# Reordering a decoder layer's vector and scalar work around its first rows, its group of index 16 and its gate groups

## The chip, the cores and the metric

The kernel runs on one core of a Trainium2 chip. The time is device microseconds for one execution. Before the change the median of three runs is 902.78 us (902.73 to 903.07). One further execution was profiled: it took 903.21 us, of which 901.4 us lie between the first and the last instruction of the core (its span). All durations below come from that one execution.

## What is computed

The reference is one decoder layer in float32 on 16 sequences of 256 rows with 256 channels. Cut to its stages:

```python
# 1. x: 4096 rows; per head of 64 channels a squared-relu attention over two fixed weights
xn = layernorm(x) * g + b
p  = square(relu(xn_heads @ k.T))           # 256 keys, 4 heads
x1 = layernorm(x + (x + p @ v))
# 2. cross attention, 16 heads of 16 channels, 16 batches of 256 queries and 256 keys
D      = clip(frac_k - frac_q, -0.2, 0.2)
logits = gamma * Q @ K.T * scale + delta * (ap * max(D, 0) + an * min(D, 0))
x2     = layernorm(x1 + softmax(logits) @ V @ Wo.T + bo)
# 3. one of 8 experts per row, a low-rank addition to a shared inner layer of 1024
e   = argmax(x2 @ gate.T + gate_b)
out = layernorm(x2 + relu(x2 @ wi.T + wi_b + lora[e]) @ wo.T + wo_b)
```

## The kernel before

All instructions are issued in an order written out by hand; each engine runs its own instructions in that order, and a wait holds back everything behind it on the same engine. The engines are PE (matrix multiply; its weight loads are shown as PEld), DVE (vector), ACT (scalar), POOL (GpSimd) and SP (here it only starts transfers).

**First stage, up to 251 us.** The rows go through in eight blocks of 512 (`rows_in`). `Block.begin` (L271) serves the first block alone. It measures mean and variance of its four tiles of 128 rows on DVE (`row_stats`, L183), takes one inverse root for all four (`scaling`, L234: `near_root`, L192, is a logarithm and an exponential on ACT; `newton`, L199, is three small DVE instructions; `scaling_of`, L238, one more), and then normalises tiles 0 and 1 on ACT (L245) and 2 and 3 on DVE (L283). `turn_first` (L288) transposes the result on PE. Ahead of these transposes stand 30 transposes of the identity (L950) whose result is not used.

**Second and third stage, 251 to 901 us.** The loop at L1062 runs over 64 groups n = 0 to 63, and two steps more. A group is one batch (n // 4) and four of its heads; og = n % 4. In step n the group `now` goes through `logits` (PE, L643, into four PSUM banks `ps_l`) and `maxima` (DVE, L658: adds the negative part of the bias, keeps the row maxima), and then `subtract` (L673) takes the maxima away, the first two heads on POOL and the last two on DVE. The group before it (`last`) is transposed on PE (`turned`, L683) and goes through the exponential on ACT (`exps`, L690), head by head: I call these e0, e1, e2 and e3. The group before that (`older`) goes through `attend` (PE, L699). For the group to come (`nxt`), `negative` (L622 on POOL, L627 on ACT) and `positive` (ACT, L634, one instruction for each bank: s0 to s3) prepare the bias.

Beside this, each step has one large piece of another batch (`pieces`, L721), whose first half is a set of matmuls and whose second half, behind `step(large_piece)`, is the copy out of PSUM:

- og = 0: `queries` (L461), matmuls L465, copied to `qT` by ACT (L481) or, where `vector` is true, by DVE (L476). In steps n = 16, 24, 32, 40, 48 and 56 it is DVE. There `late` (L1171) also puts the copy behind e2 and e3.
- og = 1: `project`. og = 2: `keys`. og = 3: `vals`, matmuls L513, copied by DVE (L521), and `Batch.turned` (L447, transposes L452, copied by ACT at L459).

`divide` (L586, on DVE at L588) scales the attention's output of the batch two before by `invs`, which a transfer has brought from DRAM; it is issued in steps with og = 0, and its result is read by `project` one step later.

From n = 15 on a third strand is woven in, the expert layer of six blocks of rows: `tb, part = divmod(n - 15, 8)`. In part 0 (n = 15, 23, 31, 39, 47, 55) `ff.turn` (L785) transposes normalised rows on PE (L790) in two halves, c0 and c1, each copied by ACT (L793). In part 1 (n = 16, 24, 32, 40, 48, 56, the gate groups) `gates` (L805) and `keep_gates` (ACT, L815) find the expert's scores. Parts 2 and 3 run the large inner matmuls (L878, L890), parts 4 to 7 the outer ones (L908).

Many of the short-lived PSUM tiles come from `tile_b` (L50). From n = 0 on it hands out three buffers in turn, two named B and one named W. So the PE instruction that fills a tile waits until the tile handed out three calls earlier has been copied out. In step 39 the order is e0, e1, `vals`, c0, c1, e2, e3, `Batch.turned`: c1 waits for the exponential of e1, and e2 for the copy of `vals`. From step 16 to 17 it is: gates, e0, e1, `queries`, e2, e3, and then e0 of step 17, which waits for the copy of `queries`.

The order of ACT in part 0 is s0, s1, exponential e0, s2, exponential e1, copy c0, copy c1, s3, exponentials e2 and e3. The parts of the step's text that set it:

```python
if last and n not in (12, 13, 14):
    last.turned(0)
    last.exps(0)
if nxt and n not in (12, 13, 14):
    nxt.positive(2)
if last and n not in (12, 13, 14):
    last.turned(1)
    last.exps(1)
```

Of the kernel before, what the change touches and what calls it, by code (L numbers as in the profile page):

```python
# [11 lines left out]
ALU = mybir.AluOpType  # L12
# [10 lines left out]
def tile_decoder_layer(ctx: ExitStack, tc: tile.TileContext, a: dict, out: bass.AP):  # L23
# [164 lines left out]
    def inv_std(mv, n):  # L188

        return newton(mv, near_root(mv, n), n)  # L190

    def near_root(mv, n):  # L192
        ln = small.tile([P, n], FP, tag="ln", name="ln")
        nc.scalar.activation(ln, mv[:, :, 1], AF.Ln, bias=epst)
        near = small.tile([P, n], FP, tag="near", name="near")
        nc.scalar.activation(near, ln, AF.Exp, scale=-0.5)
        return near

    def newton(mv, near, n):  # L199

        t = small.tile([P, n], FP, tag="sd", name="sd")
        nc.vector.scalar_tensor_tensor(t, mv[:, :, 1], EPS, near, ALU.add, ALU.mult)
        nc.vector.scalar_tensor_tensor(t, t, -0.5, near, ALU.mult, ALU.mult)
        rs = small.tile([P, n], FP, tag="rs", name="rs")
        nc.vector.scalar_tensor_tensor(rs, t, 1.5, near, ALU.add, ALU.mult)
        return rs
# [25 lines left out]
    if True:  # L232

        def scaling(mv, n):  # L234

            return scaling_of(mv, inv_std(mv, n), n)

        def scaling_of(mv, rs, n):  # L238
            nm = small.tile([P, n], FP, tag="nm", name="nm")
            nc.vector.scalar_tensor_tensor(nm, mv[:, :, 0], -1.0, rs, ALU.mult, ALU.mult)  # L240
            return rs, nm

        def scaled(dst, src, by, j):
            rs, nm = by
            nc.scalar.activation(  # L245
                dst, src, AF.Identity, bias=nm[:, j : j + 1], scale=rs[:, j : j + 1]
            )

        class Block:
# [21 lines left out]
            def begin(self):  # L271

                self.xn = p1.tile([P, 4, C], FP, tag="xn", bufs=1, name="xn")
                self.xnT = p1.tile([P, CC, 512], FP, tag="xnT", bufs=1, name="xnT")
                self.mv = small.tile([P, 4, 2], FP, tag="mv", name="mv")
                for jj in range(2):
                    self.measure(jj)
                rs, nm = scaling(self.mv, 4)
                for j in (0, 2, 1, 3):
                    if j < 2:  # L280
                        scaled(self.xn[:, j, :], self.x[:, j, :], (rs, nm), j)
                    else:
                        nc.vector.tensor_scalar(  # L283
                            self.xn[:, j, :], self.x[:, j, :], rs[:, j : j + 1],
                            nm[:, j : j + 1], ALU.mult, ALU.add,
                        )

            def turn_first(self):  # L288
# [126 lines left out]
    if True:  # L415
# [303 lines left out]
        N = len(groups)  # L719

        def pieces(n):  # L721

            b, og = divmod(n, 4)
            ahead, nxt, last, older = (
                batches[b + d] if 0 <= b + d < B else None for d in (2, 1, -1, -2)
            )
            if og == 0:
                return nxt and nxt.queries(n > 15 and n % 8 == 0), None, []
            later = nxt if nxt and nxt.b >= MADE else None
            if og == 1:  # L730
                return older and older.project(), None, [later and (lambda: later.clip("dneg"))]
            if og == 2:
                return nxt and nxt.keys(), None, [later and (lambda: later.clip("dpos"))]
            more = [ahead and ahead.load]
            if ahead:
                more.append(ahead.reload if ahead.b < MADE else ahead.fractions)
            return nxt and nxt.vals(), ahead and ahead.turned(), more

        def step(piece):
            if piece:  # L740
                next(piece, None)
# [201 lines left out]
    with tc.manual_schedule():  # L943
# [18 lines left out]
        by = [None] * (NB + 1)  # L962
# [4 lines left out]
        for tb in range(NB):  # L967
# [3 lines left out]
            mv = small.tile([P, 8, 2], FP, tag="mv8", bufs=2, name="mv8")  # L971
# [3 lines left out]
            if tb > 1:  # L975
                last = rows_in[tb - 2]
# [7 lines left out]
            if tb > 2:  # L984
                older = rows_in[tb - 3]
# [5 lines left out]
            if tb + 1 < NB:  # L991
                nxt = rows_in[tb + 1]
# [69 lines left out]
        for n in range(N + 2):  # L1062
            now, nxt, last, older = (
                groups[n + d] if 0 <= n + d < N else None for d in (0, 1, -1, -2)
            )
            large_piece, small_piece, more = pieces(n)
            tb, part = divmod(n - FIRST, 8)
            ff = rows_out[tb] if 0 <= tb < FUSED or (tb == FUSED and part < 2) else None
# [45 lines left out]
            if halved:  # L1114
                for g in range(2):
                    last.turned(g)
                    last.exps(g)
                if part == 2:
                    ff.route()
                now.subtract((nc.gpsimd, nc.vector))  # L1120
                if part == 2:
                    ff.biased()
                if done:
                    done.ready(newton(done.mv, done.near, 4))
                ff.inner(part - 2, range(0, 3))
                if part == 2:
                    ff.turn_um()
                ff.inner(part - 2, range(3, 4))
                ff.lora(part - 2, scalar=(0,))
                for g in range(4):  # L1130
                    nxt.positive(g)
                older.attend()
            else:

                if n in (12, 13, 14):
                    last.turned(0)
                    last.exps(0)
                if nxt:
                    nxt.positive(0)
                    nxt.positive(1)  # L1140
                if n in (12, 13, 14):
                    last.turned(1)
                    last.exps(1)
                    nxt.positive(2)
                    nxt.positive(3)
                if ff and part == 1 and n < N:
                    ff.keep_gates()
                if last and n not in (12, 13, 14):
                    last.turned(0)
                    last.exps(0)  # L1150
                if nxt and n not in (12, 13, 14):
                    nxt.positive(2)
                if last and n not in (12, 13, 14):
                    last.turned(1)
                    last.exps(1)
                if n == N:
                    older.attend()
                if nxt and n not in (12, 13, 14) and not (ff and part == 0):
                    nxt.positive(3)
                if prep and prep.tb:  # L1160
                    prep.rows()
            if older:
# [5 lines left out]
            if inverse:  # L1168
                inverse.invert()
            step(large_piece)  # L1170
            late = n == 1 or n % 4 == 0 and (not ff or part == 1)  # L1171
            if not late:
                step(large_piece)

# [4 lines left out]
                if nxt:  # L1179
                    nxt.positive(3)  # L1180
            divided = batches[b - 2] if og == 0 and b >= 2 else None
            if divided and ff:
                divided.divide()
            if now and not halved:
                now.subtract((nc.gpsimd, nc.gpsimd if n == 0 else nc.vector))
            if divided and not ff:
                divided.divide()
            if prep and prep.tb == 0:
                prep.rows()
# [17 lines left out]
            if n in measured:  # L1207
                j = measured.index(n)
                row_stats(hid[:, 4 * (NB - 1 - j // 4) + j % 4, :], rest_mv[:, j, :])
            if n in LATE:  # L1210
                j = LATE.index(n)
                rows_in[NB - 1 - j // 4].norm_out(by[NB], j, j % 4, nc.gpsimd)

            tb, part = divmod(n - FIRST + 4, 8)
# [117 lines left out]
```

## Time and profile before

| what | value |
|---|---|
| median of 3 runs | 902.78 us |
| the profiled execution's own time | 903.21 us |
| its span, and what lies around it | 901.4 us, 1.81 us |
| mean granted TensorE clock | 0.999 |
| DVE: subtraction L673, 63 instructions, shortest / median / longest | 1.16 / 1.22 / 2.91 us |
| DVE: division L588, 16 instructions, shortest / median / longest | 0.68 / 1.22 / 1.30 us |
| POOL: subtraction L673, shortest / median | 1.88 / 1.89 us |
| ACT: copy of queries L481, 18 instructions | 0.55 to 0.59 us each |
| DVE: copy of queries L476, 14 instructions | 0.53 to 0.55 us each |

A line of the timeline gives the start in us from the begin of the span, the time until the last of the merged instructions ended, engine, line, operation, output and inputs, the size, the count, and in brackets how long the engine was idle just before and what ended that. On one engine the next instruction can start some 0.1 us before the one ahead of it has ended. Matmul ends are modelled, so PE is best read from one start to the next.

Steps are measured here from the start of a group's logits (L643) to the start of the next group's. In the timeline these starts are at 344.48 (n = 15), 352.33 (16), 359.05 (17), 374.38 (18), and further on, for example, at 582.97 (39), 591.34 (40), 598.06 (41).

### The profile page before, as it was taken

What the parts mean: (1) busy time and instruction counts of PE and PEld (TensorE: products, weight loads), DVE (VectorE), ACT (ScalarE), POOL (GpSimd) and SP (SyncE); (2) the same over time, 40 slices, a digit from 0 to 9 for tenths busy, and PEclk for the clock granted to TensorE, in tenths of its full rate; (3) what the DMA queues carried; (4) which work ended last, traced back from release to release, by engine and by line L of the source; (5) the groups of instructions that cost most, each with busy time, mean ns of one, the idle gap of its engine ahead of it and who ended that gap; (6) DMA issues with size and microseconds to landing.
All of it is one profiled execution on the core that took longest, in us unless ns stands there. A gap on an engine that the chain in (4) does not pass through costs nothing.

```text
span 901.4 us, 19056 instructions
## 1 busy us (share of the span) xinstructions
PE 889.0 (99%) x6940; PEld 554.4 (62%) x6940; DVE 711.5 (79%) x1984; ACT 566.3 (63%) x947; POOL 390.0 (43%) x385
## 2 busy tenths in 40 slices
PE   8999999999999999999999999999999999999997
PEld 4334443434366777577668757766875786586555
DVE  5879898889779899778777887877788788778344
ACT  4766777777787878366665846655684675566111
POOL 1100212331389998435633644563464357344010
PEclk9999999999999999999999999999999999999999
DMA  5401110010001222010111202011110201111101
GB/s 141 151 1 42 53 43 25 30 48 1 14 1 55 69 70 57 13 42 21 36 47 39 49 14 67 20 37 43 43 49 13 66 19 38 42 28 44 23 2 46
DMA packets 44190, 37.01 MB, mean 41 GB/s; under 512 B 14912, under 2 KB 40000, under 8 KB 44096
## 3 DMA queue, kind: packets, MB, share of 16 engines
q1 hardware_dynamic: 43520, 35.52, 14.3%
q8 instruction: 55, 0.90, 0.4%
q14 instruction: 39, 0.32, 0.1%
q10 hardware_dynamic: 576, 0.26, 0.1%
HBM read 21.07 MB, written 6.03 MB: 30 GB/s over the span
## 4 chain that ended last, share of the span: by engine, by line
PE 91%; DVE 5%; ACT 2%; issue 1%; POOL 0%; DVEq 0%; ACTq 0%; POOLq 0%
PE ps_a L333 13%; PE ps_v L352 12%; PE ps_l L878 12%; PE ps_b L683 12%; PE ps_b L908 7%; PE ps_l L643 7%; PE ps_v L699 6%; PE ps_v L908 4%; PE ps_b L595 3%; PE ps_b L465 3%; PE ps_b L491 3%; PE ps_b L513 2%; PE ps_l L890 2%; DVE neg L658 1%; ACT ps_l L634 1%
## 5 line engine op out<-in xcount | busy, mean ns | idle before, releaser
L622 POOL TENSOR_SCALAR neg<-dneg,aneg,delta 128x512 f32<-128x512 f32 x217 | 182.5, 852 | 184.1 <-PE ps_b L683 129.4
L658 DVE CUSTOM_DVE_ANT_0 neg<-ps_l,neg 128x256 f32<-128x256 f32 x512 | 181.6, 420 | 27.1 <-PE ps_l L643 23.9
L634 ACT ACTIVATE ps_l<-dpos,apos_d 128x512 f32<-128x512 f32 x256 | 172.8, 687 | 39.1 <-DVE mx L658 34.7
L690 ACT ACTIVATE pT<-ps_b 128x512 f32<-128x512 f32 x256 | 142.8, 590 | 61.3 <-PE ps_b L683 59.2
L342 DVE TENSOR_TENSOR pr<-pr 128x1024 f32<-128x1024 f32 x128 | 154.1, 1246 | 31.5 <-ACT pr L341 31.3
L341 ACT ACTIVATE pr<-ps_a 128x1024 f32<-128x1024 f32 x128 | 124.8, 1024 | 55.7 <-PE ps_a L333 55.3
L683 PE MATMUL ps_b<-ident,neg 128*128 128x128 f32 x1024 | 138.3, 277 | 2.9 <-ACT pT L690 1.9
L683 PEld LDWEIGHTS ps_b<-ident,neg 128*128 128x128 f32 x1024 | 113.8, 141 | 36.1 <-issue 12.1
L673 POOL TENSOR_TENSOR neg<-neg,mx 128x1024 f32<-128x1024 f32 x65 | 124.3, 1912 | 18.3 <-DVE mx L658 16.5
L333 PE MATMUL ps_a<-xnT,kT 64*64 64x512 f32 x1024 | 124.0, 593 | 1.0 <-ACT xnT L318 0.4
L352 PE MATMUL ps_v<-pr,vv 64*64 64x512 f32 x1024 | 123.2, 590 | 0.0
L878 PE MATMUL ps_l<-xt,wi 128*128 128x512 f32 x248 | 111.5, 595 | 0.0
L673 DVE TENSOR_TENSOR neg<-neg,mx 128x1024 f32<-128x1024 f32 x63 | 94.6, 1502 | 0.3
L367 POOL TENSOR_TENSOR xt<-xt,half 128x512 f32<-128x512 f32 x15 | 21.6, 1437 | 153.5 <-ACT half L366 153.5
L352 PEld LDWEIGHTS ps_v<-pr,vv 64*64 64x64 f32 x1024 | 41.8, 133 | 68.9 <-issue 44.3
L333 PEld LDWEIGHTS ps_a<-xnT,kT 64*64 64x64 f32 x1024 | 38.8, 133 | 68.3 <-issue 52.4
L643 PE MATMUL ps_l<-kM,qT 32*128 32x256 f32 x1024 | 75.9, 401 | 0.0
L878 PEld LDWEIGHTS ps_l<-xt,wi 128*128 128x128 f32 x248 | 45.3, 190 | 49.0 <-issue 44.6
L407 POOL TENSOR_TENSOR hid<-hid,bo 128x256 f32<-128x256 f32 x32 | 33.4, 1059 | 81.4 <-ACT hid L245 62.6
L908 PE MATMUL ps_b<-wof,hT 128*128 128x256 f32 x304 | 68.4, 380 | 0.0
L699 PE MATMUL ps_v<-pT,vaug 128*32 128x256 f32 x1024 | 66.4, 384 | 0.0
L901 DVE TENSOR_SCALAR hT<-ps_l,wib 128x512 f32<-128x512 f32 x43 | 29.8, 745 | 44.5 <-PE ps_l L890 44.5
(131 smaller groups left out, 1089.3 us busy)
## 6 DMA issues: line engine op xcount, KB each, us to landing
cT<-in_ctxT SPq DMA_DIRECT2D x16, 256.0 KB
kM<-keys SPq DMA_DIRECT2D x128, 32.0 KB
v<-raw SPq DMA_DIRECT2D x128, 32.0 KB
invs<-rows SPq DMA_DIRECT2D x128, 32.0 KB
x<-in_x SPq DMA_DIRECT2D x7, 512.0 KB
out<-x SPq DMA_DIRECT2D x7, 512.0 KB
frow<-in_frac SPq DMA_DIRECT2D x16, 128.0 KB
wi<-in_wiT SPq DMA_DIRECT2D x1, 1024.0 KB
```

Source lines behind the costliest of these rows:

```text
L333: nc.tensor.matmul(sc[64 * k : 64 * k + 64, h, :], lhsT=kT[64 * h : 64 * h + 64, q, hf * P + 64 * k : hf * P + 64 * k + 64], rhs=self.xnT[ ...
L342: nc.vector.tensor_tensor(pr, pr, pr, ALU.mult)
L352: nc.tensor.matmul(self.acc[k][64 * h : 64 * h + 64, :], lhsT=vv[64 * k : 64 * k + 64, hf, 64 * q : 64 * q + 64], rhs=pr[64 * k : 64 * k + ...
L622: nc.gpsimd.tensor_scalar(self.neg[:, g], self.batch.dneg, aneg[:, h : h + 1], delta, ALU.mult, ALU.mult,)
L634: nc.scalar.activation(banks[g], self.batch.dpos.rearrange("p j k -> p (j k)"), AF.Copy, scale=apos_d[:, h : h + 1],)
L643: nc.tensor.matmul(banks[g][:, j * S : (j + 1) * S], lhsT=self.batch.qT[rows, self.o, j * P : (j + 1) * P], rhs=self.batch.kM[rows, self.i ...
L658: nc.vector.tensor_tensor_reduce(out=self.t[:, g, j, :], in0=banks[g][:, j * S : (j + 1) * S], in1=self.neg[:, g, j, :], scale=1.0, scalar ...
L673: eng.tensor_tensor(rows, rows, top.to_broadcast([P, 4, S]), ALU.subtract)
L683: nc.tensor.transpose(ps[:, k * S + j * P : k * S + (j + 1) * P], self.t[:, g, j, k * P : (k + 1) * P], ident,)
L690: nc.scalar.activation(self.pT[:, g, :], self.ps[g], AF.Exp)
L878: nc.tensor.matmul(self.banks[g], lhsT=wi[:, c, f * P : (f + 1) * P], rhs=self.xT[:, c, :], start=(c == 0), stop=False,)
L908: nc.tensor.matmul(ps[:, 0:C], lhsT=self.hT[f][:, j * P : (j + 1) * P], rhs=wof[:, f, :], start=(f == 0), stop=(f == FC - 1),)
```

## The change

Three edits, all of the order in which instructions are issued. The order of PE's instructions stays what it was, and no matmul is added or taken away.

1. `Block.begin` takes the inverse root of the first block in two halves: logarithm and exponential for tiles 0 and 1 are issued right behind their measuring, and ahead of the measuring of tiles 2 and 3; `newton` and `scaling_of` then run once for each half. Six small instructions on ACT and DVE become twelve.
2. In step 16 the copy of `queries` goes from DVE to ACT, and ahead of the exponentials e2 and e3 instead of behind them.
3. In part 0, ACT runs the exponential of e1 ahead of s2. In the gate groups (part 1) DVE runs `subtract` ahead of `divide`. All other steps keep their order, though the text that writes it is new.

```diff
@@ Block.begin
+                near, by = [], []
                 for jj in range(2):
                     self.measure(jj)
-                rs, nm = scaling(self.mv, 4)
+                    near.append(near_root(self.mv[:, 2 * jj : 2 * jj + 2], 2))
+                for jj in range(2):
+                    mv = self.mv[:, 2 * jj : 2 * jj + 2]
+                    by.append(scaling_of(mv, newton(mv, near[jj], 2), 2))
                 for j in (0, 2, 1, 3):
+                    rs, nm = by[j // 2]
                     if j < 2:
                         scaled(self.xn[:, j, :], self.x[:, j, :], (rs, nm), j)
                     else:
+                        k = j - 2
                         nc.vector.tensor_scalar(
-                            self.xn[:, j, :], self.x[:, j, :], rs[:, j : j + 1],
-                            nm[:, j : j + 1], ALU.mult, ALU.add,
+                            self.xn[:, j, :], self.x[:, j, :], rs[:, k : k + 1],
+                            nm[:, k : k + 1], ALU.mult, ALU.add,
                         )
@@ pieces
-                return nxt and nxt.queries(n > 15 and n % 8 == 0), None, []
+                return nxt and nxt.queries(n > 16 and n % 8 == 0), None, []
@@ the step (the old order taken out, this in its place)
+                eager = n in (12, 13, 14)
+                for act in ("e0 s0 s1 e1 s2 s3" if eager else "s0 s1 g e0 e1 s2" if ff and part == 0
+                            else "s0 s1 g e0 s2 e1 s3").split():
...
-            late = n == 1 or n % 4 == 0 and (not ff or part == 1)
+            late = n == 1 or n % 4 == 0 and (not ff or part == 1 and n > 16)
...
-            if divided and ff:
+            if divided and ff and part != 1:
                 divided.divide()
             if now and not halved:
                 now.subtract((nc.gpsimd, nc.gpsimd if n == 0 else nc.vector))
-            if divided and not ff:
+            if divided and (not ff or part == 1):
                 divided.divide()
```

More of the change, by code (lines that the diff above doesn't have):

```diff
@@ L1133, in tile_decoder_layer @@
             else:
[L1135 to L1159, printed above, removed]
+                eager = n in (12, 13, 14)
+                for act in ("e0 s0 s1 e1 s2 s3" if eager else "s0 s1 g e0 e1 s2" if ff and part == 0
+                            else "s0 s1 g e0 s2 e1 s3").split():
+                    g = int(act[1:] or 0)
+                    if act == "g":
+                        if ff and part == 1 and n < N:
+                            ff.keep_gates()
+                    elif act[0] == "s":
+                        if act == "s3" and n == N:
+                            older.attend()
+                        if nxt:
+                            nxt.positive(g)
+                    elif last:
+                        last.turned(g)
+                        last.exps(g)
                 if prep and prep.tb:
```

## The prediction, made before the change was run

> **What bounds the kernel now.** First the page's busy times:
>
> ```profile
> PE 889.0 (99%) x6940; PEld 554.4 (62%) x6940; DVE 711.5 (79%) x1984; ACT 566.3 (63%) x947; POOL 390.0 (43%) x385
> ```
>
> PE is busy 99% of the span, and the change leaves its instructions and their order alone. So time can only be won where PE stands still for another engine, and only lost where it newly does. The view of waits, of PE alone, says where (us in total, times, longest):
>
> ```profile
> PE ps_b L683 <- DVE qT L476: 0.8, 1, 0.8
> PE ps_b L790 <- ACT pT L690: 0.5, 2, 0.2
> ```
>
> One stop of 0.8 us waits for the queries' copy on DVE, two of 0.25 us for exponentials on ACT. Matmul ends are modelled, so I size stops from steps of the same part, logits to logits. Step 17 takes 15.34 us (359.05 to 374.38, rounded) where 25, 33, 41, 49 and 57 take 14.50. Part 0 takes 8.01 (31 and 55), 8.20 (23) and 8.37 (39 and 47). The gate groups take 6.72 each, 16 included: no stop there.
>
> **Edit 1, the first block.** Removed: one logarithm, one exponential, four DVE instructions on 128x4; added: two of each set on 128x2.
>
> ```profile
> 2.49 6.10 PEld L950 LDWEIGHTS ps_v<-ident 128*128 128x128 f32 x30 [2.49 <-POOL ident masks.py:199]
> ...
> 7.13 1.09 ACT L245 ACTIVATE xn<-x,nm,rs 128x256 f32<-128x256 f32 x2 [0.82 <-DVE nm L240]
> 7.13 0.73 DVE L283 TENSOR_SCALAR xn<-x,rs,nm 128x256 f32<-128x256 f32 x2
> ...
> 8.56 0.47 PEld L293 LDWEIGHTS ps_b<-ident,xn 128*128 128x128 f32 x4
> ```
>
> The normalised rows are ready at 7.13 + 1.09 = 8.22. PE's first use, at 8.56, follows the last of 30 idle transposes without a gap. After: measuring ends at 5.68 as now; eight small DVE instructions at 0.20 us start to start instead of four end at about 7.3, and two normalisations of 0.33 and 0.41 at 8.06; ACT starts its two at about 6.6 and ends at 7.7. Ready at 8.06 instead of 8.22, and hidden either way by the warming transposes: 0. Bounds: a gain of 0.05 (a delay that the view can't split off), a loss of 0.1 should the sums of small instructions run 0.5 longer than their rows. Were that cover gone, the edit would be worth 0.16.
>
> **Edit 2, step 16, with the division's new place there.** This is the stop, PE and then DVE:
>
> ```profile
> 359.05 1.15 PE L643 MATMUL ps_l<-kM,qT 32*128 32x256 f32 x16
> 361.00 0.85 PE L683 MATMUL ps_b<-ident,neg 128*128 128x128 f32 x6 [0.80 <-DVE qT L476]
> ```
>
> ```profile
> 357.65 1.15 DVE L588 TENSOR_TENSOR oT<-v,invs 128x512 f32<-128x512 f32 x1 [1.18 <-DMA invs<-rows]
> 358.73 1.21 DVE L673 TENSOR_TENSOR neg<-neg,mx 128x1024 f32<-128x1024 f32 x1
> 359.86 0.98 DVE L476 TENSOR_SCALAR qT<-ps_b,qscale,bq_s 128x256 f32<-128x256 f32 x2
> ```
>
> DVE idles 1.18 us for the transfer of invs, then divides, subtracts and copies queries until 360.85; e0 of step 17, in the queries' buffer, starts 0.15 later. Unhindered it would start 1.08 behind its logits (441: step 25 has 439.28 and 440.36), at 360.13.
>
> After, ACT makes the copy. Its queue is free after s3 (start 357.70, next 0.61 later, 358.31), the matmuls L465 are done at 358.25. From pairs of L481 elsewhere (309.01, 309.45) each takes 0.45 start to start and 0.58 to its end: copied at about 359.35, 0.63 ahead of need less the 0.15. The stop goes. Behind the copy wait e2, e3 and the last negative bias (L627), 0.48 later than now: L627 then ends near 360.9, while the exponential of e0 of step 17 could start at 360.13 + 0.76 = 360.89 (spacing of step 41). That just fits, and the buffers of e2 and e3 are wanted only at about 360.5 and 361.0.
>
> DVE after: the subtraction starts at 356.46 beside POOL's subtraction (356.36 to 358.26). The nearest row is step 15:
>
> ```profile
> 350.52 1.88 POOL L673 TENSOR_TENSOR neg<-neg,mx 128x1024 f32<-128x1024 f32 x1
> 350.61 2.90 DVE L673 TENSOR_TENSOR neg<-neg,mx 128x1024 f32<-128x1024 f32 x1
> ```
>
> It ends 1.10 behind POOL's, so here at 359.36; the division, no longer first, takes 0.68 (its shortest row) to 359.96; the wait for invs lies under the subtraction. The maxima of 17 can start then, and in steady steps they start 1.29 behind the logits, at 360.34. Nothing is late. Value: 15.34 - 14.50 = **0.84 gained**; bounds 0.87 (the whole stop) and 0 (if the later exponentials hold PE instead).
>
> **Edit 3a, part 0: e1 ahead of s2.** Step 39, PE, ACT and the values' copy on DVE:
>
> ```profile
> 588.58 0.60 PE L790 MATMUL ps_b<-ident,x 128*128 128x128 f32 x4
> 589.43 0.66 PE L790 MATMUL ps_b<-ident,x 128*128 128x128 f32 x4 [0.25 <-ACT pT L690]
> 589.92 1.04 PE L683 MATMUL ps_b<-ident,neg 128*128 128x128 f32 x8
> ```
>
> ```profile
> 587.70 0.58 ACT L690 ACTIVATE pT<-ps_b 128x512 f32<-128x512 f32 x1
> 588.18 0.68 ACT L634 ACTIVATE ps_l<-dpos,apos_d 128x512 f32<-128x512 f32 x1
> 588.79 0.58 ACT L690 ACTIVATE pT<-ps_b 128x512 f32<-128x512 f32 x1
> 589.26 0.58 ACT L793 COPY xt<-ps_b 128x512 f32<-128x512 f32 x1
> ```
>
> ```profile
> 588.88 0.68 DVE L521 COPY vaug<-ps_b 128x512 f32<-128x512 f32 x1
> ```
>
> c1 could start 0.44 behind c0 (step 31), at 589.02, but waits for e1's exponential (ends 589.37). With e1 at 588.18 that ends at 588.77: the wait goes. What is late next: e2 needs the values' copy (L521 ends 589.56; in step 31 e2 starts 0.05 behind it), so e2 starts at 589.60 instead of 589.92, 0.32 won. Then s3: ACT's sum of work is unchanged, the copy of c0 starts at 589.28, of c1 at 589.76, s3 at 590.24 with end 590.94; the logits now start 0.04 behind s3's end, so 590.98, and by PE's own spacing at 591.00: 0.34 won. Step 47 has the same stops and limits: 0.34. Step 23 (c1 held 0.24, e2 limited at 430.91 against 431.14, s3 ending 432.27): 0.26. Step 15 (c1 held 0.17, values' copy done 350.69): 0.17. In steps 31 and 55 ACT waits 0.72 and 0.88 for PE ahead of c0's copy; s2 moves into that: 0. Sum **1.11 gained**; bounds 1.3 (all of what c1 waits) and 0.5 (if s3, which has only 0.02 to spare, comes 0.1 later in each).
>
> **Edit 3b, gate groups 24 to 56: subtraction ahead of division.** Two instructions of DVE change places ahead of the queries' copy, which DVE keeps here:
>
> ```profile
> 438.98 0.98 DVE L476 TENSOR_SCALAR qT<-ps_b,qscale,bq_s 128x256 f32<-128x256 f32 x2
> ...
> 440.36 0.88 PE L683 MATMUL ps_b<-ident,neg 128*128 128x128 f32 x6
> ```
>
> The copy ends at 439.96, 0.40 ahead of its user, 0.25 more than the 0.15 it needs. In step 40 division (595.40, 1.29) and subtraction (596.62, 1.21) end at 597.83; POOL's subtraction ends at 596.15. Swapped: subtraction until 596.15 + 1.10 = 597.25, division 597.17 + 0.68 = 597.85. 0.02 later, inside the 0.25: 0. The project matmuls that read the division come 10 us later. Bounds: 0 and the loss of the third rival.
>
> [...]
>
> **The sum.** 0 + 0.84 + 1.11 + 0 = 1.95 us. The profiled execution's 903.21 would become 901.26. It lies 0.43 above the median of 902.78; less 1.95 the median becomes **900.83**, or 0.22% faster. A measurement of this kernel can tell about 0.2% (1.81 us) from no change, so the forecast sits close to that line.
>
> **The rivals.**
> 1. *Part 0 keeps its stop under another name*: c1 no longer waits, but s3 or the values' copy holds the logits. For it: s3 already ends 0.04 ahead of the logits in 23, 39, 47. Against: ACT's sum does not grow. Gain 0.84 + 0.2 = 1.0: 901.8. Chance 0.13.
> 2. *The stop of step 17 moves to ACT*: the later exponentials and L627 hold e0's exponential and the expert's transposes. For it: the fit is exact. Against: e2 of 16 is ready 0.9 ahead of its buffer's next use. Then only edit 3a counts: 901.7. Chance 0.09.
> 3. *Slower: in the five gate groups DVE's subtraction is shut out.* If POOL's subtraction starts only when DVE's does, DVE's takes 2.90 (step 15's row) instead of 1.85; with the division the copy ends at 595.40 + 2.90 + 0.60 + 0.97 = 599.87 in step 40 against 598.74, and PE's e0 comes at 600.02, not 599.13: 0.89 each, 4.45 in all, less 1.95: 905.3. It decides once POOL's subtraction ends 0.25 us later than now. For it: step 16 has POOL at that point. Against: in 24 to 56 POOL starts 1.14 ahead, and nothing moves it. Chance 0.05.
> 4. *Nothing comes of it*: stops shown by the trace are the profile's own. 902.8. Chance 0.04.
> 5. *More*: a step behind a mended one closes up too. 900.2. Chance 0.05.
>
> The forecast (900.4 to 901.3) has 0.64. Range 900.3 to 902.0: forecast and rivals 1 and 2, 0.86, the least that reaches 0.8. About 0.7 of the forecast's share and rival 5 lie below 900.97: faster 0.50; same 0.45; slower 0.05.
>
> **What would show it.** Right: the wait of PE on qT gone and step 17 at 14.5; steps 39 and 47 at 8.03, 23 at 7.94, 15 at 7.68; the gate groups at 6.72; the first transposes still at 8.56. Wrong: PE waiting for ACT in step 17, for s3 ahead of the logits of 24, 40 or 48, or for qT in any of 25 to 57.

## The result, and the profile after

The changed kernel takes 900.58 us in the median of 9 runs (900.37 to 901.41); the kernel before, run beside it, 902.90 us (902.73 to 903.39). The ratio is 0.9975, with a 95% interval from 0.9964 to 0.9985: 2.32 us faster, where 1.95 had been forecast. The profiled execution took 900.42 us, its span is 898.6 us: 2.79 and 2.76 less than in the profiled execution of before. That the profiles differ by 0.5 more than the medians is part of the story below.

Lines of the changed kernel stand 6 further down from L289 on (L299 is the first rows' transposes, L649 the logits, L689 the transposes, L696 the exponentials, L487 the queries' copy). The page's busy times, and PE's view of waits:

```profile
PE 887.7 (99%) x6940; PEld 553.3 (62%) x6940; DVE 713.0 (79%) x1986; ACT 567.2 (63%) x951; POOL 390.3 (43%) x385
```

```profile
PE ps_b L689 <- ACT pT L696: 1.8, 4, 0.5
PE ps_a L339 <- ACT xnT L324: 0.4, 1, 0.4
```

Neither row is new. The second read 0.4, 1, 0.4 before too, and the first, in the view of before, was:

```profile
PE ps_b L683 <- ACT pT L690: 1.9, 5, 0.5
```

The wait on qT and the two stops of the expert's transposes (L790 before, L796 now) are gone from the view. Step by step, logits to logits, and for the start up to the first logits:

| stretch | before | after | won | forecast |
|---|---|---|---|---|
| start of the first rows' transposes | 8.67 | 7.65 | 1.02 | 0 |
| from there to the logits of group 0 | 245.95 | 245.97 | -0.02 | 0 |
| step 7 | 6.51 | 6.43 | 0.08 | 0 |
| steps 15, 23, 39, 47 (part 0) | 7.85, 8.20, 8.37, 8.37 | 7.73, 8.01, 8.09, 8.10 | 0.86 | 1.11 |
| steps 31 and 55 (part 0) | 8.01 | 8.01 | 0 | 0 |
| step 17 | 15.34 | 14.50 | 0.84 | 0.84 |
| gate groups 16, 24 to 56 | 6.72 | 6.72 | 0 | 0 |

All other steps agree within 0.03. The table's 2.78 are the span's 2.76. The part of the groups came out near the forecast. In this pair of executions the largest single term was one that I had put at zero: the start.

**Step 17.** PE after: the first transposes of step 17 start 1.08 behind its logits, with no wait.

```profile
357.85 1.15 PE L649 MATMUL ps_l<-kM,qT 32*128 32x256 f32 x16
358.93 1.09 PE L689 MATMUL ps_b<-ident,neg 128*128 128x128 f32 x8
```

ACT and DVE after:

```profile
357.12 1.02 ACT L487 ACTIVATE qT<-ps_b,bq_s,qscale 128x256 f32<-128x256 f32 x2
358.02 1.10 ACT L696 ACTIVATE pT<-ps_b 128x512 f32<-128x512 f32 x2
358.97 0.75 ACT L633 ACTIVATE neg<-dneg,aneg_d 128x512 f32<-128x512 f32 x1
359.68 0.60 ACT L696 ACTIVATE pT<-ps_b 128x512 f32<-128x512 f32 x1
```

```profile
355.31 2.96 DVE L679 TENSOR_TENSOR neg<-neg,mx 128x1024 f32<-128x1024 f32 x1
358.19 0.68 DVE L594 TENSOR_TENSOR oT<-v,invs 128x512 f32<-128x512 f32 x1
```

The copy ends 0.79 ahead of its user, the two exponentials and the negative bias follow without a gap, and the exponential of e0 (359.68) starts just behind the bias: the tight fit that the prediction named is there, and it holds. The subtraction takes 2.96 beside POOL's, as the row of step 15 had said, and the division 0.68 without a wait for invs.

**Step 39.** PE, ACT and DVE's values' copy after:

```profile
586.35 1.04 PE L796 MATMUL ps_b<-ident,x 128*128 128x128 f32 x8
587.37 1.10 PE L689 MATMUL ps_b<-ident,neg 128*128 128x128 f32 x8
588.30 0.60 PE L458 MATMUL ps_b<-ident,hid 128*128 128x128 f32 x4
```

```profile
585.46 1.06 ACT L696 ACTIVATE pT<-ps_b 128x512 f32<-128x512 f32 x2
586.42 0.69 ACT L640 ACTIVATE ps_l<-dpos,apos_d 128x512 f32<-128x512 f32 x1
587.03 1.08 ACT L799 COPY xt<-ps_b 128x512 f32<-128x512 f32 x2
```

```profile
586.64 0.67 DVE L527 COPY vaug<-ps_b 128x512 f32<-128x512 f32 x1
```

The eight transposes of c0 and c1 (L796) run in one piece. What is late next is what the prediction said: e2 starts 0.05 to 0.06 behind the end of the values' copy (587.31).

**The start.** The same stretch, 6 to 7 us, in the view by windows, before and then after (the third column is PE's busy time, with the number of its instructions):

```profile
6.00:7.00 1.00, 1.00 (x6) 1.00 (x5) 0.55 (x4) 0.28 (x2) 0.00 (x0) 1.00 1.07 223
```

```profile
6.00:7.00 1.00, 1.00 (x10) 1.00 (x9) 0.86 (x6) 0.87 (x4) 0.00 (x0) 1.00 1.02 206
```

PE runs the same 30 idle transposes in both, from 2.49 us on, first one each 0.213 us and then one each 0.109. The spacing changes behind the transpose at 8.31 us in this execution of before, and behind the one at 6.17 in this one of after. The trace's record of PE's clock begins there, at full: at 8.37 and at 6.28. It has nothing ahead of that, so the views by windows give a clock of 1.00 (the eighth column) in both; the rise is read from the record's begin and the spacing together. So the idle transposes end a full microsecond earlier. No instruction of PE was moved, and in the other profiles that begin with the same transposes the clock was full from 5.25 to 8.24 us with the old order of the roots and from 6.39 to 8.30 with the new one. So it is not the change that brings the early clock. What the change does is to let the kernel use it. The first rows are ready:

```profile
6.37 1.09 ACT L245 ACTIVATE xn<-x,nm,rs 128x256 f32<-128x256 f32 x2
...
7.08 0.74 DVE L289 TENSOR_SCALAR xn<-x,rs,nm 128x256 f32<-128x256 f32 x2
```

Tiles 0 and 1 are done at 7.46 and tiles 2 and 3 at 7.82, just in time for transposes at 7.65 to 7.97. With the old order tile 1 came at 8.22, and PE wants it second.

### The profile page after: what moved, and what is told of

The parts are those of the page before. It is cut to its first block, busy times and chain, and to the rows that moved or that the text cites. A ratio compares the mean times of both kernels' runs of the same rounds, so it can differ in the third digit from the quotient of the medians.

```text
span 898.6 us, 19061 instructions
## 1 busy us (share of the span) xinstructions
PE 887.7 (99%) x6940; PEld 553.3 (62%) x6940; DVE 713.0 (79%) x1986; ACT 567.2 (63%) x951; POOL 390.3 (43%) x385
## 4 chain that ended last, share of the span: by engine, by line
PE 97%; DVE 1%; ACT 1%; issue 0%; POOL 0%; DVEq 0%; ACTq 0%; POOLq 0%
PE ps_b L689 13%; PE ps_a L339 13%; PE ps_v L358 12%; PE ps_l L884 12%; PE ps_l L649 8%; PE ps_b L914 7%; PE ps_v L705 7%; PE ps_v L914 5%; PE ps_b L601 3%; PE ps_b L497 3%; PE ps_b L471 3%; PE ps_b L519 3%; PE ps_l L896 2%; PE ps_b L811 1%; PE ps_b L458 1%; PE ps_b L796 1%
## 5 line engine op out<-in xcount | busy, mean ns | idle before, releaser
L696 ACT ACTIVATE pT<-ps_b 128x512 f32<-128x512 f32 x256 | 142.3, 591 | 59.3 <-PE ps_b L689 57.2
L689 PE MATMUL ps_b<-ident,neg 128*128 128x128 f32 x1024 | 138.5, 277 | 2.0 <-ACT pT L696 1.8
L689 PEld LDWEIGHTS ps_b<-ident,neg 128*128 128x128 f32 x1024 | 113.6, 141 | 35.9 <-issue 12.4
L679 DVE TENSOR_TENSOR neg<-neg,mx 128x1024 f32<-128x1024 f32 x63 | 99.1, 1574 | 0.6
L649 PE MATMUL ps_l<-kM,qT 32*128 32x256 f32 x1024 | 75.9, 401 | 0.0
```

The costliest lines, as they stand in the source:

```text
L649: nc.tensor.matmul(banks[g][:, j * S : (j + 1) * S], lhsT=self.batch.qT[rows, self.o, j * P : (j + 1) * P], rhs=self.batch.kM[rows, self.i ...
L679: eng.tensor_tensor(rows, rows, top.to_broadcast([P, 4, S]), ALU.subtract)
L689: nc.tensor.transpose(ps[:, k * S + j * P : k * S + (j + 1) * P], self.t[:, g, j, k * P : (k + 1) * P], ident,)
L696: nc.scalar.activation(self.pT[:, g, :], self.ps[g], AF.Exp)
```

## Experiments

The theory, formed from the two traces: the steps' gains are what was predicted, and edit 1 has a worth that varies, since its cover, the idle transposes, has a length that varies with the moment at which PE's clock rises. The rival for the start is the prediction's own: edit 1 is worth nothing, and the extra comes from elsewhere. "Steps" below are read from each run's own profile, so the start doesn't touch them. The first four runs have one execution each, the others 8 to 11, beside the kernel before (medians 902.77 to 902.91).

**Edit 2 without the division's new place.** Kernel before, with

```diff
-                return nxt and nxt.queries(n > 15 and n % 8 == 0), None, []
+                return nxt and nxt.queries(n > 16 and n % 8 == 0), None, []
...
-            late = n == 1 or n % 4 == 0 and (not ff or part == 1)
+            late = n == 1 or n % 4 == 0 and (not ff or part == 1 and n > 16)
```

> Edit 2 without the division's new place: in step 16 ScalarE copies the queries ahead of the last two exponentials, VectorE still divides ahead of subtracting and still waits for invs. Theory (the queries' buffer alone held step 17): step 17 takes 14.50 as in the changed kernel, since the subtraction still ends at 359.94 and the maxima of 17 need VectorE only at 360.34. Rival (the division that waits for a transfer has to go behind as well): step 17 keeps a stop of some 0.3 or more, at the maxima.

Step 17 took 14.50. DVE waited 1.55 us for invs and ended its subtraction at 359.90; the maxima of 17 started at 360.29, behind the logits and not behind DVE. The theory holds. The division's move is not needed for this gain.

**The copy on ACT, behind the exponentials.** Only the first of these two lines is changed.

> In step 16 ScalarE copies the queries, but behind the last two exponentials; division ahead of subtraction. Theory: the copy starts at about 359.7 and ends at 360.7, so the transposes of step 17 still wait, 0.6 to 0.75 of the 0.84 stays: step 17 takes 15.1 to 15.3. Rival (it matters that the copy leaves VectorE, not where it stands): 14.50.

Step 17 took 15.20. ACT's copy, and PE behind it:

```profile
359.86 1.02 ACT L481 ACTIVATE qT<-ps_b,bq_s,qscale 128x256 f32<-128x256 f32 x2
```

```profile
361.02 1.07 PE L683 MATMUL ps_b<-ident,neg 128*128 128x128 f32 x8 [0.66 <-ACT qT L481]
```

The wait has changed its owner and kept most of its length. So it is the place ahead of e2 and e3 that frees PE, not the engine alone. (An earlier place with the copy left on DVE was not tried.) This run also shows the start with the old roots and an early clock (full from 5.25 us); PE's first transposes:

```profile
8.38 0.33 PE L293 MATMUL ps_b<-ident,xn 128*128 128x128 f32 x1 [1.07 <-ACT xn L245]
8.87 0.55 PE L293 MATMUL ps_b<-ident,xn 128*128 128x128 f32 x3 [0.16 <-ACT xn L245]
```

PE is free early and waits 1.07 us for tile 0 and then for tile 1, the wait that the profile of before could not show. (The first tile of x also landed late here, 4.04 us instead of 3.45.)

**The division behind the subtraction, alone.** The last two pairs of changed lines in the diff.

> Division behind subtraction in the gate groups alone, queries' copy as before. Theory: nothing. Step 16's copy of queries ends at 360.9 as before and step 17 takes 15.3 to 15.4; in 24 to 56 the copy ends within 0.05 of where it did and the steps stay 6.72 and 14.50. Rival (VectorE's subtraction is shut out by GpSimd's): steps 25 to 57 grow by up to 0.89 each. Second rival (the new order alone frees step 17): 14.50 there.

Step 17 took 15.36, steps 24 to 56 took 6.72, steps 25 to 57 took 14.50: nothing, as the theory has it. DVE in step 16:

```profile
356.28 2.85 DVE L673 TENSOR_TENSOR neg<-neg,mx 128x1024 f32<-128x1024 f32 x1
359.06 0.68 DVE L588 TENSOR_TENSOR oT<-v,invs 128x512 f32<-128x512 f32 x1
359.66 0.98 DVE L476 TENSOR_SCALAR qT<-ps_b,qscale,bq_s 128x256 f32<-128x256 f32 x2
```

What the division no longer waits for invs, the subtraction now waits beside POOL's (2.85 us, where it took 1.21 before). In step 24 the pair ends at 438.85 and the copy at 439.75, 0.6 ahead of the maxima that follow. The prediction's third rival (DVE shut out in five groups) doesn't occur.

**e1 ahead of s2, alone.**

```diff
-                if nxt and n not in (12, 13, 14):
+                if nxt and n not in (12, 13, 14) and not (ff and part == 0):
                     nxt.positive(2)
                 if last and n not in (12, 13, 14):
                     last.turned(1)
                     last.exps(1)
+                if nxt and ff and part == 0:
+                    nxt.positive(2)
```

> Edit 3a alone: in part 0 the second exponential ahead of the third positive bias. Theory: the steps of the changed kernel, 7.73, 8.00, 8.01, 8.09, 8.10, 8.01 for 15, 23, 31, 39, 47, 55, all others as before (17: 15.34). Rival (what part 0 gives needs the other edits, since they come ahead of 23 to 55): 15 as changed, the rest between before and after.

Part 0 took 7.73, 8.01, 8.01, 8.10, 8.09, 8.01, as in the changed kernel: these steps don't need the other edits. But step 17 took 15.46, where 15.34 was expected: PE's stop there is 0.92 us instead of 0.80, and DVE waits 1.25 us for invs instead of 1.18. Steps 15 to 17 together take 29.91 us; before, they took 29.90. So the 0.12 won in step 15 is lost again in step 17 while that stop stands: alone, this edit is worth 0.74 in the steps, and 0.86 only together with edit 2.

**Edit 1 alone, and the change without it.** The first hunk of the diff put into the kernel before; and taken out of the changed one.

> Edit 1 alone, put into the kernel before. Theory (the cover of the warming transposes varies): PE's clock rose to full 8.37 us into the profiled execution of before and 6.28 us into that of after; the earlier it rises, the sooner the 30 warming transposes end, and then the first rows' root is on the path, with at most 8.67 - 8.28 = 0.39 us to be won by an early clock with the old order and 1.0 with the new. So executions spread over about 1.0 us instead of 0.66, the shortest is 0.6 below the shortest of before (902.1), the median 902.3 to 902.8; all steps of the groups as before (part 0: 8.20, 8.01, 8.37, 8.37, 8.01; step 17: 15.34). Rival (the prediction's own step, edit 1 is worth nothing): median and shortest as before, 902.9 and 902.7.

> The changed kernel with edit 1 undone, edits 2 and 3 kept. Theory (varying cover): only what the steps give, 0.83 in step 17, 0.87 in part 0 and perhaps 0.08 in step 7: 902.9 - 1.75 = 901.15 in the median, shortest 901.0, spread 0.66 as before. Rival (edit 1 is worth nothing, and the 0.5 that the change gave beyond its steps comes from elsewhere in it): 900.6 as the whole change.

Alone: median 902.56 (902.20 to 903.49, 11 runs) against 902.91 (902.61 to 903.33, 31 runs), ratio 0.9997 with an interval of 0.9988 to 1.0006. The interval doesn't exclude zero; the spread is 1.29 against 0.72, and four of the eleven runs lie at 902.42 or below, where none of the 31 does. Without it: 901.14 (901.03 to 901.52), ratio 0.9981 (0.9973 to 0.9990), 1.77 below before; its steps give 1.67. Between it and the whole change lie 0.56 in the medians. (The whole change ran at another time; the kernel before had 902.90 beside it and 902.91 here.) So the extra 0.5 is edit 1's: the medians put it at 0.35 to 0.56, with the 0.08 of step 7 in it, and the rival falls. One step went against the expectation: with edit 1 alone, step 34 took 14.20 in the profile where it took 14.06 before.

The profiles also show what the start hangs on. In five of the eight with the old order of the roots, PE waits for the rows, and the last of its eight first transposes starts 5.53 to 5.54 us behind the first measuring of x; in the other three the idle transposes last longer than that. With the new order PE waits for the rows in one profile only (the last run below, with 16 matmuls), and there it is 4.90. So edit 1 is worth 0.64 at the start when the cover is out of the way, and nothing when the cover outlasts both. The first measuring of x itself starts at 3.31 to 4.04 us in the 14 profiles, when its transfer has landed. That moves the start as well: the clock is not the only thing in which executions differ.

**The cover made shorter and longer.** `WARM` is the number of idle transposes, 30 in both kernels.

```diff
-WARM = 30
+WARM = 24      # and 40
```

> The kernel before with 24 idle transposes instead of 30; the result doesn't depend on them. Theory (varying cover): with the cover cut to 7.7 us even at half clock, the old order of the roots always binds, its second tile ready at 8.28: every execution like the short ones of before, 902.7 to 902.9, little spread, unless the clock rises later than 8.3 and the first real transposes run at half speed (0.1 us each). Rival (the first rows are not on the path): 0.6 less than before, 902.3, as six transposes of 0.11 us are left out.

> The changed kernel with 24 idle transposes instead of 30. Theory (varying cover): the roots bind at about 7.88 in every execution: 900.4, the shortest of the changed kernel, for nearly all, median 0.1 to 0.2 below the changed kernel's 900.58, and 2.4 below e3. Rival (first rows not on the path): 1.8 below e3.

> The kernel before with 40 idle transposes instead of 30. With the clock full at 5.3 to 9 us they end at 8.2 to 10 us, so the first rows are ready before PE is free, in nearly every execution and with either order of the roots. Theory (varying cover): later than before by 0.5 to 1.1 us: 903.4 to 904.0. Rival (the length of the warming doesn't matter since another start-up wait hides it): 902.9.

> The changed kernel with 40 idle transposes. Theory (varying cover): with the cover always long enough, edit 1 is worth nothing at the start, and this lies below e9 by the steps alone, 1.7 to 1.8 us (part 0 0.87, step 17 0.83, step 7 0.08). Rival (edit 1 is worth 0.4 to 0.6 by itself, whatever the cover): 2.2 to 2.4 below e9.

| idle transposes | kernel before | changed kernel | between the medians |
|---|---|---|---|
| 24 | 902.82 (902.64 to 903.14) | 900.63 (900.36 to 900.87) | 2.19 |
| 30 | 902.90 (902.73 to 903.39) | 900.58 (900.37 to 901.41) | 2.32 |
| 40 | 903.50 (902.74 to 904.26) | 902.08 (901.60 to 902.54) | 1.42 |

With 24 in the kernel before, six transposes fewer won nothing to speak of: the roots bind, as the theory has it. In the changed kernel the upper end went from 901.41 to 900.87, but the median did not fall by the 0.1 to 0.2 expected. Its profiled execution, at 900.78 one of the longer ones, shows one reason: the clock rose only at 8.30, and the first real transposes, at 7.67, 7.89, 8.10 and 8.31, came 0.21 us apart, not 0.11. With 40 the difference shrinks by about 0.9; by the steps it should be 1.7 to 1.8, and 1.42 came out. The kernels spread over 1.5 and 0.9 us there, so this pair speaks for the theory in sign and leaves the size open. In neither of its two profiles does PE wait for the first rows. The 9 us that the expectation allows the clock was an estimate; 8.37 is the latest that a profile shows.

**A try at a faster version.** Put into the changed kernel, with `WARM` at 32 and then at 16: the idle work as plain matmuls of a tile of ones that DVE sets at once, so that PE begins near 1 us; and in part 0 DVE copies the values ahead of the raw outputs.

```diff
+        blank = const.tile([P, P], FP, name="blank")
+        nc.vector.memset(blank, 1.0)
...
-            nc.tensor.transpose(idle[:, j % 4 * P : (j % 4 + 1) * P], ident, ident)
+            nc.tensor.matmul(idle[:, j % 4 * P : (j % 4 + 1) * P], lhsT=blank, rhs=blank, start=True, stop=True)
...
-            if older:
+            swap = ff and part == 0
+            if older and not swap:
                 older.keep()
...
                 step(large_piece)
+            if older and swap:
+                older.keep()
```

> A try at a faster version: the changed kernel with the warming done by 32 plain 128x128 matmuls of a tile of ones that VectorE sets at the very start, so that PE begins near 0.8 us instead of 2.49; and in part 0 VectorE copies the values ahead of the raw outputs. Theory (varying cover): the clock rises before the roots are done at 7.8 in nearly every execution, the transposes start at 7.65 to 7.9 at full clock, so 900.3 to 900.4 with a spread under 0.5, if the clock doesn't fall again in PE's pause of up to 2 us; steps 39 and 47 go from 8.10 to 8.02 and take another 0.15, so 900.2. Rival (the start's spread is not the clock's): spread 1.0 and median as the changed kernel, 900.5.

> As e11, with 16 plain matmuls, since a float32 matmul of 128x128 showed as two passes of 0.21 us at half clock: 32 passes from 1.05 us on end by 7.9 at the latest. Theory (varying cover): the clock is full between 4 and 8 us, the first rows' transposes start at 7.65 to 7.9 in nearly every execution, and the execution takes 900.2 to 900.5 with a spread under 0.5, against 900.4 to 901.4 for the changed kernel. Rival (PE's pause of up to 2 us ahead of the transposes lets the clock fall again, or keeps it from rising): transposes at 0.21 us each, 0.5 to 0.8 longer, 901.0 or more, spread about 1. Steps 39 and 47: 8.02.

With 32 matmuls: 903.46 (902.48 to 903.70). A miss: the trace has 64 records for 32 matmuls, two for each, so the cover ended at 9.7 us. With 16: **900.28** (900.04 to 900.73, 8 runs), ratio 0.9971 (0.9961 to 0.9982), 0.3 below the changed kernel's median, with a spread of 0.69 instead of 1.04 (under 0.5 had been expected). But the kernel before was at 902.77 beside this run and at 902.90 beside the changed kernel, so 2.49 us were won against 2.32, and the two intervals overlap almost wholly: that this version is faster than the changed kernel is not shown. The clock was full from 5.59 (the 4 to 8 us expected were an estimate), and the transposes started at 7.03 to 7.79, as their rows came in. Steps 39 and 47 fell from 8.09 and 8.10 to 8.01, so the values' copy was what still held them. Step 34 rose from 14.06 to 14.20 and step 16 from 6.72 to 6.75, in both runs, which takes the gain back. That the swap of DVE's copies makes step 34 longer is not shown: the run with edit 1 alone, which swaps nothing, has the same 14.20. Why it grows stays open.

## Why the prediction was right, and where it was off

- **The time and the sign** were right: 900.83 forecast, 900.58 measured, inside 900.3 to 902.0. A part of that is luck: two errors of opposite sign, 0.25 too much for part 0 and 0.35 to 0.56 too little for edit 1, partly cancel.
- **Step 17** (0.84 forecast): 0.84. The mechanism was the predicted one: ACT's copy stands ahead of the buffer's need, and the delayed exponentials just fit. That the division's place added nothing here was in the working (the maxima need DVE only at 360.34) but was not drawn as a conclusion; the run without it settles it.
- **Part 0** (1.11 forecast): 0.86. The mechanism and the limits were right (c1 no longer held, then the values' copy; nothing in 31 and 55). The size of the term was off by 0.05 to 0.07 in each of 15, 23, 39 and 47. In the trace of before, the transposes behind a stop follow closer: from e2 to the next piece 0.87 us in step 39, against 0.93 in the undisturbed step 31 and in step 39 after. I took the 0.87 over as if it would stay. In step 39 e2 itself starts 6.63 behind the logits, just where the prediction had it, so the miss lies in this spacing alone: PE had already made up 0.06 of the stop right behind it.
- **Gate groups 24 to 56** (0): 0. In step 24, with the division moved alone, the subtraction took 1.71 us, where 1.85 had been computed for step 40.
- **Edit 1** (0 forecast, a gain of 0.05 as the bound): this is the step that failed. The prediction said "hidden either way by the warming transposes", and held that cover to be as long as in the one execution shown. The sign that it gave, the first transposes still at 8.56, came out as 7.54. The cover's length depends on when the clock rises: the last of the 30 idle transposes starts at 7.04 us where the clock is full from 5.25, and at 8.56 where it is full from 8.37. In the 14 profiles of this study the clock rises 2.8 to 5.9 us after PE's first instruction, and the execution profiled before, at 5.9, was the latest of all. Why it rises when it does, no run here shows. The step also said "Were that cover gone, the edit would be worth 0.16", from the last tile's time (8.22 against 8.06). But PE wants the tiles in the order 0, 1, 2, 3, and with the old roots tile 1 is the late one, so three of the first four transposes still have to run when it is ready; with the new roots only that of tile 3 has. With the cover gone, the last of the eight starts 5.54 behind the first measuring of x with the old roots (24 idle transposes) and 4.90 with the new ones (16 matmuls): 0.64, four times the 0.16. Last, tiles 2 and 3 were ready at 7.82 and not at 8.06: the eight small DVE instructions began at 5.62, just before the measuring had ended, and came 0.18 apart in the mean, not 0.20.
- **Step 7** (not forecast): 0.08. The step takes 6.42 to 6.43 in all six profiles with edit 1, whatever else they change, and 6.51 in all eight without it. ACT in this step, before and then after:

```profile
298.03 0.69 ACT L634 ACTIVATE ps_l<-dpos,apos_d 128x512 f32<-128x512 f32 x1 [1.21 <-issue]
299.01 0.69 ACT L634 ACTIVATE ps_l<-dpos,apos_d 128x512 f32<-128x512 f32 x1 [0.29 <-ACT ps_l L634]
```

```profile
297.33 1.30 ACT L640 ACTIVATE ps_l<-dpos,apos_d 128x512 f32<-128x512 f32 x2 [1.49 <-issue]
```

  The two positive biases come 0.98 apart before and 0.62 after, behind a pause that no semaphore explains ("issue"). The gain goes with edit 1, which puts two more instructions into ACT's stream ahead of this place and four more into DVE's; how that shortens the step was not tried, and stays open.
- Of the rivals, none came about at its price. A part of the first did, and the sum had it: the values' copy still holds steps 39 and 47, at 8.09 and 8.10 where step 31 takes 8.01. "More" (900.2) was named for the wrong place: it was the start that had something to give, not a step behind a mended one.

## What to carry to other kernels

Where an edit is costed at nothing because other work covers it, ask what sets the length of the cover and whether one execution can show its range; a warm-up whose speed hangs on a clock that rises at its own time (2.8 to 5.9 us after PE's first instruction here) is not a fixed cover. A spread of the runs (0.66 us here, before) is a reason to look, though here the landing of x (first measuring at 3.31 to 4.04 us) had its part in it. Where PE waits for a shared buffer, look at which copy releases it and what stands ahead of that copy on its engine: with the copy on ACT, the place in the queue made 0.70 of the 0.84 us, and the change of engine by itself only 0.14. Size a stop by whole steps against undisturbed ones, and look at the spacing behind the stop as well as at the stop. And try each edit alone: what one wins can be lost again at a stop that another one removes.

## What the runs showed of the hardware

- PE's clock rose to full 2.8 to 5.9 us after PE's first instruction, in executions with the same first instructions (at 5.25 us in the run with the copy behind the exponentials, at 8.37 in the profile of before); the idle transposes went from 0.213 to 0.109 us each there.
- A pause of PE of 1.07 us ahead of the first transposes did not bring the clock down: the transposes behind it were 0.11 us apart (the run with the copy behind the exponentials).
- 32 plain float32 matmuls of 128x128 left 64 records, two for each, 0.21 us apart ahead of the clock's rise (the run with 32 matmuls), where 30 transposes of the same size left 30.
- DVE's subtraction in step 16 of the changed kernel started 0.01 us behind POOL's (355.31 and 355.30), took 2.96 us and ended 1.09 behind it; the one of step 39 took 1.21.
